# Reordering the passage between two stages of a recurrent layer, and one place for raw weights

## The chip, the cores and the metric

The kernel runs on one core of one Trainium2 chip. The metric is the device time of one execution in microseconds (us). The kernel before takes 1391.1 us, the median of three runs (1390.11 to 1394.08). The engines of the core are named here as in the profile: PE is TensorE (matrix products), DVE is VectorE, ACT is ScalarE, POOL is GpSimd and SP is SyncE. DMA transfers are issued through queues of SP, ACT and POOL. SBUF is the on-chip memory that all engines work on, PSUM the small memory that TensorE writes.

## The reference

The input x has 2048 tokens of 512 numbers. The layer is a gated attention over four lags with a feed-forward gate beside it:

```python
xn = _layernorm(x)
q, k, v = (causal_dwconv(silu(xn @ W), conv_w) for each of q, k, v)   # 16 heads of 128, 4 taps
z, a, b = xn @ Wz, xn @ Wa, xn @ Wb
q, k = rotary(q), rotary(k)
q, k = q / max(norm(q), 1e-12), k / max(norm(k), 1e-12)
out = zeros_like(v)
for s in range(4):                                     # lag s: shifted by s tokens
    attn = einsum('bshd,bshd->bsh', q, lag(k, s)) / sqrt(128)
    gate = sigmoid(lag(a, s) * b)
    out = out + (attn * gate)[..., None] * lag(v, s)
out = out * rsqrt(mean(out * out, over all 2048 channels) + 1e-6) * norm_w * silu(z)
s = out @ Wout
g = silu(relu(xn @ sign(up).T * up_scale) @ sign(down).T * down_scale * output_scale)
x = x + s * g
```

The lines above shorten the reference; every operation is kept.

## The kernel before, in words

Heads are handled in 8 pairs (p, 256 channels each) and tokens in 4 blocks (b, 512 tokens each). The kernel has two stages.

**Stage 1** (to about 760 us) goes over blocks and pairs with one `step` (L508) each: the products of q and k, their convolutions, the rotation (`turn`), the four lagged products of q and k (`product`, into the tiles `pr`), and, as matrix products with a matrix of ones per head, their sums (`sum_dots`) and the sums of squares (`sum_squares`). The feed-forward products (`ups`, `downs`) run beside on TensorE. Once per block, `norms`, `norms_in_rows` and `coefficients` (L470 to L504) make the weights of the four lags for all heads and store them in DRAM as `co_dram[b]`. `norms_in_rows` moves norms between partitions by eight small DMAs on SP's queue (L493, L494), and `coefficients` ends with the store (L504).

**Stage 2** (from about 740 us, main loop at L1056) goes over 16 values of i: 8 pairs for the first 1024 tokens, then 8 for the second 1024. For each i there are

- a projection pv for v (`raw_values`) and a projection pz for z (`gated_outputs`), both through `project_forms`: three products of split operands, first d (16 matmuls), then, after a scaling of the result on ACT (L819), h and m (32 matmuls);
- v's convolution (`values`): ACT makes the first tap (L856), DVE adds three taps for both halves of the channels, six operations;
- for both halves h of the tokens `weighted`: the rows of coefficients are spread over the partitions by DMA (`bc`, four transfers of 256 KB on SP's queue), DVE multiplies them with v (te, twice), adds them, and adds once more to o;
- `gating` (o times silu of z, normed by `norm_w`) and `output_projection` (po) for earlier i.

The weights come as raw 512 KB tiles (`load_raw`, L608), which `split_raw` (L618) divides into three parts: h on ACT (L630), m and d on DVE (L631, L632), then a scaling of m on ACT (L633). Three pools take the parts in turn (`pool_of`, L799): `vs` (opened only after stage 1, L1035), `wp` (the place of stage 1's weights) and `wfp` (the place of the feed-forward's raw weights). v of i is turn 2i, z of i turn 2i + 1. In `vs` and `wfp` a raw tile takes one of the pool's four places of its tag; for `wp` it has a place in `vs` (tag `wraw`).

What sets the order: every instruction issued through `pe`, `dve`, `pool`, `act` and `sp` (the class `InOrder`, L45) keeps the order of the program on its engine or queue; those through `nc.scalar`, `nc.sync` and `nc.gpsimd` are placed by a scheduler, and each engine runs its list in order in the end. Tiles that share a pool's tag share memory: a write waits until the last reader of the tile before is done. `att.close()` (L1033) ends the memory of stage 1's pool `qks`, which `vs` takes over; so the first tiles of `vs` wait for what lies there, such as the coefficients' `rk` and `rq`.

The passage between the stages is written out at L1022 to L1049: the first projection of v, the sums left over from stage 1, `norms` and `norms_in_rows` for the last block, the first projection of z, v's second weights, v's first convolution, `coefficients`, the end of `qks`, two first te tiles, the raw weights of z 1, and the loads of `down_scale` and `out_scale`. The raw weights of v 0 and z 0 are loaded during the last block of stage 1 (p = 4 and p = 6, L780 to L787); z 0 is split inside the last step, between its convolution and its rotation (the argument `between`, L768).

Of the kernel before, what the change touches and what calls it, by code (L numbers as in the profile page):

```python
# [17 lines left out]
P = 128  # L18
# [40 lines left out]
def recurrent_layer(ctx: ExitStack, tc: tile.TileContext, a: dict, out: bass.AP):  # L59
# [40 lines left out]
    wp = ctx.enter_context(tc.tile_pool(name="wp", bufs=3))  # L100
    wfp = ctx.enter_context(tc.tile_pool(name="wfp", bufs=4, side="right"))
# [5 lines left out]
    pr_tiles = [qks.tile([P, LAGS, TB], F32, tag=f"pr{n}", name=f"pr{n}") for n in range(2)] + [spare]  # L107
# [128 lines left out]
    def gate_products(b):  # L236
# [12 lines left out]
        ab = qks.tile([P, TB], F32, tag="ab", name=f"ab_sb{b}", bufs=1)  # L249
# [127 lines left out]
    def queries(p, b):  # L377

        if p or b:
            load("q", p, b)  # L380
        q = qks.tile([P, LAGS, 2, TB], F32, tag="q", name=f"q_{p}_{b}", bufs=1)
        q0 = q[:, LAGS - 1]
        convolve(0, p, raw_of(qks, "q", p, b), q0)
        return q
# [223 lines left out]
    def load_raw(pool, n, i, by=None):  # L608
        if pool is not wp:
            w = pool.tile([P, KC, 2 * P], F32, tag="wf", name=f"w{n}_{i}", bufs=4)  # L610
        elif i:
            w = vs.tile([P, KC, 2 * P], F32, tag="wraw", name=f"w{n}_{i}")
        else:
            w = wfp.tile([P, KC, 2 * P], F32, tag="wf", name=f"w{n}_{i}", bufs=4)
        (by or (sp if i else nc.sync)).dma_start(w, a[f"w{n}"][i % NP])
        w_raws[n, i] = pool, w

    def split_raw(n, i):  # L618
        pool, w = w_raws.pop((n, i))
        h, m, d = (  # L620
            pool.tile(
                [P, KC, 2 * P],
                F32R,
                tag="w" if pool is wp else "wf",
                name=f"w{n}_{i}_{t}",
                bufs=3 if pool is wp else 4,
            )
            for t in "hmd"
        )
# [18 lines left out]
    with tc.tile_pool(name="pre", bufs=1, side="right") as pre:  # L648
# [91 lines left out]
        for b in range(NTB):  # L740
            for p in range(NP):
# [13 lines left out]
                else:  # L755

                    def first_downs():
# [4 lines left out]
                    end = n == len(groups) - 1  # L762
                    step(
                        p,
                        b - 1,
                        first_downs,
                        lambda: downs(b, g, 2, TC),
                        (lambda: split_raw("z", 0)) if end else None,  # L768
                    )
# [9 lines left out]
                if b == NTB - 1:  # L779
                    if p == 4:  # L780
                        load_raw(wfp, "v", 0)
                    if 1 < p < 5:
                        hold_form(0, (2, 0, 1)[p - 2])
                        fill_form(0, (2, 0, 1)[p - 2], nc.sync)
                    if p == 6:
                        split_raw("v", 0)
                        load_raw(wp, "z", 0)  # L787
                        for i in (2, 0, 1):
                            hold_form(1, i)
                            fill_form(1, i, nc.sync)  # L790
# [8 lines left out]
    def pool_of(n, i):  # L799
        return (vs, wp, wfp)[rounds[n, i] % 3]  # L800
# [67 lines left out]
    def weighted(i, h, v):  # L868
        s, p = divmod(i, NP)
        b = 2 * s + h  # L870
        n = f"_{p}_{b}"
        parts = []
        for lo in range(0, LAGS, 2):
            bc = vr.tile([P, 2, TB], F32, tag="bc", name=f"bc{lo}" + n, bufs=3)
            for hd in range(2):
# [27 lines left out]
    def load_wo(i, by=None, tag="wo", bufs=2):  # L903
        wo = take(tag) or (by or vs).tile([P, 2, HID], F32, tag=tag, name=f"wo_{i}", bufs=bufs)
# [65 lines left out]
    def load_squares(s):  # L970
        ss = squares[s] = [
            take("y") or vs.tile([P, TB], F32, tag="y", name=f"ss{s}_{h}", bufs=2) for h in range(2)
# [5 lines left out]
    def roots(s, more=None):  # L978
        so = sums.tile([P, TB], F32, tag="squares", name=f"so{s}")
        row = take("g") or vs.tile([P, TB], F32, tag="g", name=f"row{s}", bufs=2)  # L980
# [40 lines left out]

    raw = raw_values(0)  # L1022
    for work in sums_at.pop(NP * NTB):
        work()
    sum_dots()
    norms(last)
    norms_in_rows(last)
    z0 = gated_outputs(0)
    load_raw(wfp, "v", 1)
    split_raw("v", 1)  # L1030
    v0 = values(0, raw)
# [16 lines left out]
    sp.dma_start(down_scale, a["down_scale"].partition_broadcast(P))  # L1048
    sp.dma_start(out_scale, a["out_scale"].partition_broadcast(P))  # L1049
# [6 lines left out]
    for i in range(n_all + 1):  # L1056
# [23 lines left out]
        if i:  # L1080
# [29 lines left out]
    g_last += [vs.tile([P, 2, HID], F32, tag="wf", name=f"g_last{n}", bufs=4) for n in (2, 3)]  # L1110
# [89 lines left out]
```

## Time and profile before

| what | value |
|---|---|
| median of three runs | 1391.1 us (1390.11 to 1394.08) |
| profiled execution, its own time | 1392.0 us |
| span of the profiled execution | 1390.2 us |
| granted TensorE clock, mean | 0.983 |
| TensorE (PE) busy | 1329.1 us, 96% |
| VectorE (DVE) busy | 1189.0 us, 86% |
| ScalarE (ACT) busy | 841.9 us, 61% |
| GpSimd (POOL) busy | 204.9 us, 15% |
| DMA moved | 285.43 MB, mean 205 GB/s |

The profile page cuts the span into 40 slices of 34.8 us and gives the busy share of each engine as a digit (9 is 90% or more). A line of the timeline is: start in us, duration in us, engine (SPq, ACTq and POOLq are the queues' issues), line, operation, output<-inputs, shapes, the number of instructions joined, and in brackets the idle time of the engine just before with what ended it. A line of the waits is: engine, tile and line that waited, what it waited for, the sum in us, how often, and the longest. Since operations pass through the class `InOrder`, many of them carry its line, L53, and are told apart by their tiles. Buffer numbers are left out of tile names, so `wz_h` is the h part of some z weight.

### The profile page before, as it was taken

What the parts mean: (1) busy time and instruction counts of PE and PEld (TensorE: products, weight loads), DVE (VectorE), ACT (ScalarE), POOL (GpSimd) and SP (SyncE); (2) the same over time, 40 slices, a digit from 0 to 9 for tenths busy, and PEclk for the clock granted to TensorE, in tenths of its full rate; (3) what the DMA queues carried; (4) which work ended last, traced back from release to release, by engine and by line L of the source; (5) the groups of instructions that cost most, each with busy time, mean ns of one, the idle gap of its engine ahead of it and who ended that gap; (6) DMA issues with size and microseconds to landing.
All of it is one profiled execution on the core that took longest, in us unless ns stands there. A gap on an engine that the chain in (4) does not pass through costs nothing. (4 is left out here: it accounts for less than half of the span.)

```text
span 1390.2 us, 13682 instructions
## 1 busy us (share of the span) xinstructions
PE 1329.1 (96%) x4586; PEld 793.0 (57%) x4586; DVE 1189.0 (86%) x1091; ACT 841.9 (61%) x1484; POOL 204.9 (15%) x266
## 2 busy tenths in 40 slices
PE   9999999999999999999997657999999999999996
PEld 6555555555555555555554545666666566666652
DVE  6998999988979888799885489999886898899875
ACT  7566757676577666555655455666655666666541
POOL 1121111112211131111110000111111111111110
PEclk9999999999999999999999879999999999999998
DMA  9969786999889998989784276676889776688876
GB/s 312 359 180 221 191 229 193 217 215 239 228 218 253 221 214 221 255 222 255 169 218 81 76 182 164 151 187 149 181 212 296 173 176 172 180 191 207 206 202 196
DMA packets 100143, 285.43 MB, mean 205 GB/s; under 512 B 16804, under 2 KB 17188, under 8 KB 89576
## 3 DMA queue, kind: packets, MB, share of 16 engines
q1 hardware_dynamic: 66424, 174.43, 41.0%
q0 software_dynamic: 32784, 103.83, 37.8%
q10 hardware_dynamic: 864, 6.29, 1.2%
q8 instruction: 36, 0.59, 0.2%
q14 instruction: 35, 0.29, 0.1%
HBM read 167.05 MB, written 74.47 MB: 174 GB/s over the span
## 5 line engine op out<-in xcount | busy, mean ns | idle before, releaser
L53 PE MATMUL pq<-xn,wq 128*128 128x512 f32 (+1 forms) x528 | 225.6, 580 | 0.6 <-ACT rk L294 0.6
L53 PE MATMUL po<-wo,o 128*128 128x512 f32 x512 | 222.5, 592 | 3.3 <-DVE o L53 3.3
L53 PE MATMUL pk<-xn,wk 128*128 128x512 f32 x512 | 224.9, 592 | 0.0
L53 PEld LDWEIGHTS po<-wo,o 128*128 128x128 f32 x512 | 97.0, 190 | 121.0 <-issue 115.0
L53 PEld LDWEIGHTS pq<-xn,wq 128*128 128x128 f32 x528 | 99.6, 190 | 111.0 <-issue 105.2
L53 PEld LDWEIGHTS pk<-xn,wk 128*128 128x128 f32 x512 | 97.1, 190 | 109.7 <-issue 107.0
L53 DVE SCALAR_TENSOR_TENSOR v<-rv,conv_w,v 128x1024 f32<-128x1024 f32 x96 | 122.0, 1284 | 29.0 <-ACT v L856 26.7
L53 DVE TENSOR_TENSOR te<-v,bc 128x2048 f32<-128x2048 f32 x62 | 139.3, 2287 | 8.5 <-DMA bc<-co_dram 8.1
L53 DVE SCALAR_TENSOR_TENSOR q<-q,turns 128x1024 f32<-128x1024 f32 (+1 forms) x128 | 127.3, 1016 | 4.4 <-ACT q L53 2.2
L53 PE MATMUL pv<-xf,wv_h 128*128 128x512 f32 x256 | 102.2, 399 | 9.6 <-ACT pv L819 9.6
L53 PE MATMUL pf<-down,hid_hi 128*128 128x512 f32 x256 | 108.8, 425 | 0.0
L53 PE MATMUL ph<-xs_h,up 128*128 128x512 f32 x256 | 107.9, 422 | 0.0
L53 PE MATMUL pv<-xf,wv_m 128*128 128x512 f32 x256 | 101.4, 396 | 1.4 <-DMA xf<-forms_dram 1.4
L53 PE MATMUL pf<-down,hid_lo 128*128 128x512 f32 x256 | 100.5, 393 | 0.6 <-DVE hid_lo L53 0.6
L53 PE MATMUL pz<-xf,wz_h 128*128 128x512 f32 x256 | 100.6, 393 | 0.1
L53 DVE SCALAR_TENSOR_TENSOR k<-rk,conv_w,k 128x512 f32<-128x512 f32 x128 | 96.3, 752 | 4.5
L53 DVE SCALAR_TENSOR_TENSOR q<-rq,conv_w,q 128x512 f32<-128x512 f32 x128 | 96.3, 752 | 4.5
L53 PE MATMUL ph<-xs_m,up 128*128 128x512 f32 x256 | 100.0, 391 | 0.0
L53 PE MATMUL pz<-xf,wz_m 128*128 128x512 f32 x256 | 99.9, 390 | 0.0
L53 DVE TENSOR_TENSOR pr<-q,k 128x2048 f32<-128x2048 f32 x44 | 99.6, 2285 | 0.3
L53 PE MATMUL pz<-xf,wz_d 128*128 128x512 f32 x256 | 65.6, 411 | 27.6 <-issue 20.5
L53 DVE SCALAR_TENSOR_TENSOR k<-rk,conv_w,tap 128x512 f32<-128x512 f32 x64 | 48.0, 750 | 48.2 <-ACT tap L360 48.1
(170 smaller groups left out, 2263.0 us busy)
## 6 DMA issues: line engine op xcount, KB each, us to landing
bc<-co_dram SPq DMA_DIRECT2D x128, 256.0 KB
wq<-in_wq_dram SPq DMA_DIRECT2D x32, 512.0 KB
wk<-in_wk_dram SPq DMA_DIRECT2D x32, 512.0 KB
sq<-sq POOLq DMA_DIRECT2D x32, 512.0 KB, 8.3
f_dram<-f POOLq DMA_DIRECT2D x64, 256.0 KB, 8.6
o_dram<-o POOLq DMA_DIRECT2D x30, 512.0 KB, 7.8
s_dram<-part POOLq DMA_DIRECT2D x56, 256.0 KB, 6.5
up<-up_signs SPq DMA_DIRECT2D x12, 1024.0 KB
```

Of the source, the lines that this page charges most:

```text
L53: return self.tc.keep_in_program_order(getattr(self.engine, op)(*args, **kwargs))
```

## The change

- `pr` tiles of stage 1 move from `qks` to `xnp`, a pool that lives on; stage 2's te tiles take their places.
- A new pool `qp` with one place holds q in stage 1, then the three parts of every third weight as one tile (in place of the parts in `vs`), and at the end `g_last` and the last squares of o.
- The raw weights of v 0 and z 0 are loaded at p = 2 of the last block, v 0 is split at p = 5, v 1 is loaded at p = 6. The split of z 0 moves out of the last step to behind it.
- In the passage, v's first convolution, the parts of v 1, the first rows, the first te products (`spread`) and the parts of z 1 come ahead of the coefficients. `weighted` is divided into `load_rows`, `spread` and the rest for this.
- In the main loop, raw weights for `qp` and `wp` go through one place (`wraw` in `vs`, one buffer), loaded by `load_behind` behind the rows of each half. Raw weights for `wfp` are loaded as before.
- `down_scale` and `out_scale` are loaded through ACT's queue instead of SP's. The tile `ab` shares a place with `x_in` (or `gate`), and `take` with its first tiles goes.

```diff
     wp = ctx.enter_context(tc.tile_pool(name="wp", bufs=3))
+    qp = ctx.enter_context(tc.tile_pool(name="qp", bufs=1))
     wfp = ctx.enter_context(tc.tile_pool(name="wfp", bufs=4, side="right"))
...
     spare = xnp.tile([P, LAGS, TB], F32, tag="spare", name="spare")
-    pr_tiles = [qks.tile([P, LAGS, TB], F32, tag=f"pr{n}", name=f"pr{n}") for n in range(2)] + [spare]
+    pr_tiles = [xnp.tile([P, LAGS, TB], F32, tag=f"pr{n}", name=f"pr{n}") for n in range(2)] + [spare]
 
...
             )
-        ab = qks.tile([P, TB], F32, tag="ab", name=f"ab_sb{b}", bufs=1)
+        ab = qks.tile([P, TB], F32, tag="x_in" if b else "gate", name=f"ab_sb{b}", bufs=1)
         nc.scalar.copy(ab, chunks)
...
             load("q", p, b)
-        q = qks.tile([P, LAGS, 2, TB], F32, tag="q", name=f"q_{p}_{b}", bufs=1)
+        q = qp.tile([P, LAGS, 2, TB], F32, tag="q", name=f"q_{p}_{b}")
         q0 = q[:, LAGS - 1]
...
 
-    def load_raw(pool, n, i, by=None):
-        if pool is not wp:
-            w = pool.tile([P, KC, 2 * P], F32, tag="wf", name=f"w{n}_{i}", bufs=4)
-        elif i:
-            w = vs.tile([P, KC, 2 * P], F32, tag="wraw", name=f"w{n}_{i}")
-        else:
-            w = wfp.tile([P, KC, 2 * P], F32, tag="wf", name=f"w{n}_{i}", bufs=4)
-        (by or (sp if i else nc.sync)).dma_start(w, a[f"w{n}"][i % NP])
+    def load_raw(pool, n, i):
+        at, tag, bufs = (wfp, "wf", 4) if pool is wfp else (qks, "x_in", 1) if i < 2 else (vs, "wraw", 1)
+        w = at.tile([P, KC, 2 * P], F32, tag=tag, name=f"w{n}_{i}", bufs=bufs)
+        (sp if i else nc.sync).dma_start(w, a[f"w{n}"][i % NP])
         w_raws[n, i] = pool, w
...
         pool, w = w_raws.pop((n, i))
-        h, m, d = (
-            pool.tile(
-                [P, KC, 2 * P],
-                F32R,
-                tag="w" if pool is wp else "wf",
-                name=f"w{n}_{i}_{t}",
-                bufs=3 if pool is wp else 4,
-            )
-            for t in "hmd"
-        )
+        shape = [P, KC, 2 * P]
+        if pool is qp:
+            parts = qp.tile([P, 3, *shape[1:]], F32R, tag="q", name=f"w{n}_{i}_hmd")
+            h, m, d = (parts[:, t] for t in range(3))
+        else:
+            tag, bufs = ("wf", 4) if pool is wfp else ("w", 3)
+            h, m, d = (pool.tile(shape, F32R, tag=tag, name=f"w{n}_{i}_{t}", bufs=bufs) for t in "hmd")
         nc.scalar.activation(h, w, AF.Copy, scale=LOW)
...
 
-                    end = n == len(groups) - 1
-                    step(
-                        p,
-                        b - 1,
-                        first_downs,
-                        lambda: downs(b, g, 2, TC),
-                        (lambda: split_raw("z", 0)) if end else None,
-                    )
+                    step(p, b - 1, first_downs, lambda: downs(b, g, 2, TC))
                 if n + 1 < len(groups):
...
                 if b == NTB - 1:
-                    if p == 4:
+                    if p == 2:
                         load_raw(wfp, "v", 0)
+                        load_raw(wp, "z", 0)
                     if 1 < p < 5:
...
                         fill_form(0, (2, 0, 1)[p - 2], nc.sync)
-                    if p == 6:
+                    if p == 5:
                         split_raw("v", 0)
-                        load_raw(wp, "z", 0)
+                    if p == 6:
+                        load_raw(wfp, "v", 1)
                         for i in (2, 0, 1):
...
     def pool_of(n, i):
-        return (vs, wp, wfp)[rounds[n, i] % 3]
+        return (qp, wp, wfp)[rounds[n, i] % 3]
 
...
 
-    def weighted(i, h, v):
+    def load_rows(i, h):
         s, p = divmod(i, NP)
         b = 2 * s + h
-        n = f"_{p}_{b}"
-        parts = []
+        bcs = []
         for lo in range(0, LAGS, 2):
-            bc = vr.tile([P, 2, TB], F32, tag="bc", name=f"bc{lo}" + n, bufs=3)
+            bc = vr.tile([P, 2, TB], F32, tag="bc", name=f"bc{lo}_{p}_{b}", bufs=3)
+            bcs.append(bc)
             for hd in range(2):
...
                 )
+        return bcs
+
+    def spread(i, h, v, bcs):
+        s, p = divmod(i, NP)
+        n = f"_{p}_{2 * s + h}"
+        parts = []
+        for lo, bc in zip(range(0, LAGS, 2), bcs):
             v0 = v[:, :, h * TB + lo : h * TB + lo + TB]
             v_lags = bass.AP(v0.tensor, v0.offset, [v0.ap[0], [1, 2], *v0.ap[1:]])
-            te = take(f"te{lo}") or vs.tile([P, 2, 2, TB], F32, tag=f"te{lo}", name=f"te{lo}" + n)
+            te = xnp.tile([P, 2, 2, TB], F32, tag=f"pr{lo // 2}", name=f"te{lo}" + n)
             dve.tensor_tensor(te, v_lags, bc.unsqueeze(2).to_broadcast([P, 2, 2, TB]), ALU.mult)
...
         dve.tensor_tensor(parts[0], parts[0], parts[1], ALU.add)
-        o = take("oz") or vs.tile([P, 2, TB], F32, tag="oz", name="o" + n, bufs=6)
-        dve.tensor_tensor(o, parts[0][:, 0], parts[0][:, 1], ALU.add)
+        return parts[0]
+
+    def weighted(i, h, part):
+        s, p = divmod(i, NP)
+        b = 2 * s + h
+        n = f"_{p}_{b}"
+        o = vs.tile([P, 2, TB], F32, tag="oz", name="o" + n, bufs=6)
+        dve.tensor_tensor(o, part[:, 0], part[:, 1], ALU.add)
         os[i, h] = o
         if h and i == NSB * NP - 1:
-            o2 = vs.tile([P, 2, TB], F32, tag="wf", name="o2" + n, bufs=4)
+            o2 = end_places[2]
         else:
...
 
+    split_raw("z", 0)
     raw = raw_values(0)
...
     sum_dots()
+    load_raw(qp, "z", 1)
     norms(last)
-    norms_in_rows(last)
     z0 = gated_outputs(0)
-    load_raw(wfp, "v", 1)
-    split_raw("v", 1)
     v0 = values(0, raw)
+    split_raw("v", 1)
+    first_rows = [load_rows(0, h) for h in range(2)]
+    norms_in_rows(last)
+    first_part = spread(0, 0, v0, first_rows[0])
+    split_raw("z", 1)
     coefficients(last)
...
     vs = ctx.enter_context(tc.tile_pool(name="vs", bufs=1))
-    firsts = {}
-
-    def first(tag, shape, name, bufs=1):
-        firsts[tag] = vs.tile(shape, F32, tag=tag, name=name, bufs=bufs)
-
-    def take(tag):
-        return firsts.pop(tag, None)
-
-    first("te0", [P, 2, 2, TB], "te0_first")
-    first("te2", [P, 2, 2, TB], "te2_first")
-    load_raw(pool_of("z", 1), "z", 1)
     down_scale = vs.tile([P, HID], F32, tag="down_scale", name="down_scale")
-    sp.dma_start(down_scale, a["down_scale"].partition_broadcast(P))
-    sp.dma_start(out_scale, a["out_scale"].partition_broadcast(P))
+    nc.scalar.dma_start(down_scale, a["down_scale"].partition_broadcast(P))
+    nc.scalar.dma_start(out_scale, a["out_scale"].partition_broadcast(P))
+
+    def load_behind(n, i):
+        if i < 2 or i >= n_all or pool_of(n, i) is wfp:
+            return
+        for _ in range(2):
+            n, i = ("z", i) if n == "v" else ("v", i + 1)
+            if i < n_all and pool_of(n, i) is not wfp:
+                load_raw(pool_of(n, i), n, i)
+                return
 
...
                 split_raw("v", i + 1)
-            if i + 2 < n_all:
+            if i + 2 < n_all and pool_of("v", i + 2) is wfp:
                 load_raw(pool_of("v", i + 2), "v", i + 2)
...
             load_raw(pool_of("v", 2), "v", 2)
+        if i == n_all - 1:
+            ends = qp.tile([P, 4, 2, HID], F32, tag="q", name="ends")
+            end_places = [ends[:, n] for n in range(3)]
         v = values(i, raw) if i else v0
         for h in range(2):
-            weighted(i, h, v)
+            rows_of_h = load_rows(i, h) if i else first_rows[h]
+            load_behind("vz"[h], i + 1)
+            weighted(i, h, spread(i, h, v, rows_of_h) if i or h else first_part)
             if ended:
...
                 load_end(2 * (i - NP - 3) + h)
-            if not h and i + 1 < n_all:
+            if not h and 0 < i < n_all - 1:
                 split_raw("z", i + 1)
-            if not h and i + 2 < n_all:
+            if not h and i + 2 < n_all and pool_of("z", i + 2) is wfp:
                 load_raw(pool_of("z", i + 2), "z", i + 2)
...
     ]
-    g_last += [vs.tile([P, 2, HID], F32, tag="wf", name=f"g_last{n}", bufs=4) for n in (2, 3)]
+    g_last += end_places[:2]
     parts = []
```

Where `take(...) or` stood before a tile, the tile alone is left.

More of the change, by code (lines that the diff above doesn't have):

```diff
@@ L784, in recurrent_layer @@
                         fill_form(0, (2, 0, 1)[p - 2], nc.sync)
+                    if p == 5:
+                        split_raw("v", 0)
                     if p == 6:
-                        split_raw("v", 0)
-                        load_raw(wp, "z", 0)
+                        load_raw(wfp, "v", 1)
                         for i in (2, 0, 1):
@@ L903, in load_wo @@
     def load_wo(i, by=None, tag="wo", bufs=2):
-        wo = take(tag) or (by or vs).tile([P, 2, HID], F32, tag=tag, name=f"wo_{i}", bufs=bufs)
+        wo = (by or vs).tile([P, 2, HID], F32, tag=tag, name=f"wo_{i}", bufs=bufs)
         sp.dma_start(wo, a["wo"][i % NP])
@@ L971, in load_squares @@
         ss = squares[s] = [
-            take("y") or vs.tile([P, TB], F32, tag="y", name=f"ss{s}_{h}", bufs=2) for h in range(2)
+            vs.tile([P, TB], F32, tag="y", name=f"ss{s}_{h}", bufs=2) for h in range(2)
         ]
@@ L979, in roots @@
         so = sums.tile([P, TB], F32, tag="squares", name=f"so{s}")
-        row = take("g") or vs.tile([P, TB], F32, tag="g", name=f"row{s}", bufs=2)
+        row = vs.tile([P, TB], F32, tag="g", name=f"row{s}", bufs=2)
         ss = squares.pop(s)
@@ L1025, in recurrent_layer @@
     sum_dots()
+    load_raw(qp, "z", 1)
     norms(last)
+    z0 = gated_outputs(0)
+    v0 = values(0, raw)
+    split_raw("v", 1)
+    first_rows = [load_rows(0, h) for h in range(2)]
     norms_in_rows(last)
-    z0 = gated_outputs(0)
-    load_raw(wfp, "v", 1)
-    split_raw("v", 1)
-    v0 = values(0, raw)
+    first_part = spread(0, 0, v0, first_rows[0])
+    split_raw("z", 1)
     coefficients(last)
```

## Prediction

> **What bounds the kernel now.** I read the page's busy shares first, then its 40 slices, then TensorE's waits, then the timelines of the engines that those waits name.
>
> ```profile
> PE 1329.1 (96%) x4586; PEld 793.0 (57%) x4586; DVE 1189.0 (86%) x1091; ACT 841.9 (61%) x1484; POOL 204.9 (15%) x266
> ...
> PE   9999999999999999999997657999999999999996
> ```
>
> TensorE works 1329.1 of 1390.2 us. The 61 us that it stands idle lie almost all in slices 22 to 24, which is 740 to 850 us, the passage from stage 1 (queries and keys) to stage 2 (values and gates). The waits of TensorE between 740 and 860 us give their causes:
>
> ```profile
> PE pz L53 <- issue: 20.5, 1, 20.5
> PE pz L53 <- DVE wz_d L53: 7.1, 1, 7.1
> PE pv L53 <- ACT pv L819: 7.0, 1, 7.0
> PE pv L53 <- DVE wv_d L53: 5.9, 1, 5.9
> ```
>
> Four gaps, 40.5 us together. After each the clock is low for a while: sixteen matmuls of one form take 6.11 us after the long gap, 3.93 us without one, in the timeline of TensorE:
>
> ```profile
> 814.72 6.11 PE L53 MATMUL pz<-xf,wz_d 128*128 128x512 f32 x16 [20.53 <-issue]
> 828.03 3.93 PE L53 MATMUL pv<-xf,wv_d 128*128 128x512 f32 x16
> ```
>
> So a gap of seven or more microseconds costs about 2.2 us (6.11 - 3.93) on top. The Trainium skill ("TensorE: Matmul & The Clock Gate", part 1 on the clock gate) has the array at half clock until it has been busy for about 3.4 us; by that rule the surcharge would be an estimated 1.7 us per gap, and the total below would move by about 1 us. I use the row.
>
> What stands behind the gaps is seen on ScalarE, VectorE and SyncE's queue:
>
> ```profile
> 736.14 1.06 ACT L630 ACTIVATE wz_h<-wz 128x1024 fp32r<-128x1024 f32 x1 [7.68 <-DMA wz<-in_wz_dram]
> ...
> 808.58 1.06 ACT L630 ACTIVATE wz_h<-wz 128x1024 fp32r<-128x1024 f32 x1 [6.15 <-DMA wz<-in_wz_dram]
> ...
> 1073.93 1.06 ACT L630 ACTIVATE wv_h<-wv 128x1024 fp32r<-128x1024 f32 x1 [4.33 <-DMA wv<-in_wv_dram]
> ```
>
> ```profile
> 790.15 0.33 SPq L504 DMA_DIRECT2D co_dram<-rk  x1
> ...
> 796.93 0.64 SPq L53 DMA_DIRECT2D wz<-in_wz_dram  x1
> ```
>
> ```profile
> 803.74 2.29 DVE L53 TENSOR_TENSOR te_first<-v,bc 128x2048 f32<-128x2048 f32 x1 [13.62 <-DMA bc<-co_dram]
> ```
>
> The coefficients' last work holds memory that stage 2 needs. Only when they are stored (790.15) are the rows and z's second raw weights loaded. VectorE then stands for 13.62 us, and z's second parts are ready only at 814.6.
>
> **The change, part by part.** The program orders of the two kernels, with the durations of these rows, give the following.
>
> (1) z's first raw weights are loaded four steps earlier, and only h is made before the last products. The wait of 7.68 us ahead of wz_h goes, as does that wz_h (1.06 us) from ScalarE's way to rk's eviction, and 2.45 us (1.22 + 1.23) of m and d on VectorE from before the turn. The products end near 746 instead of 756.3. TensorE's 7.02 us and its ramp go: v's first projection ends near 751 instead of 760.0. The loads themselves I cost at nothing, since they lie beside slices in which PE reads 9 and are used steps later; without that cover each would cost the 3.5 us of a load on a quiet queue (v's second weights, issued 773.46, used 776.94).
>
> (2) v's second raw weights come two steps before the end instead of behind eight rq/rk issues, so their parts (1.06 + 1.23 + 1.22 us) are ready near 765 instead of 780.5. The 5.90 us wait and its ramp go: pv 1 runs from about 765.5 to 777.
>
> (3) z's second parts go to the third place, freed by the last products. VectorE, with r's reciprocal done at 768.6, does two te products and their sum (3 x 2.29 = 6.9) to 775.5, then m and d (2.45) to 778. pz 1 starts near 778 instead of 814.72: the 20.53 us gap shrinks to about 1.
>
> (4) The coefficients now come behind this. Five of the eight rq/rk issues stand on SyncE behind a row load that waits for the first te. The three coefficient operations (3 x 0.68) end near 781.5, the store takes 2.0 us, and only then is there memory for o and for the raw weights of v 2 and z 2. VectorE from 783.5: o 1.2, te of the second half with sum and o 8.0, two gatings 2.5, parts of v 2 2.5, v 1's convolution 7.8, te and o of the next half 8.0, parts of z 2 2.5. That sums to 816.0. With two short waits for the loads I take 818 for the start of pz 2, against 846.29 (the gap of 7.1 us there ends with VectorE's d). Here is the whole gain of the passage: **28 us**. It is no more, since a gap of some 9.5 us is left ahead of pv 2, whose weights wait for the store. Bounds: 34, if the store needs no wait for the rq/rk copies; 18, if the last rq/rk copy and the raw weights each land like the slowest load shown (11.65 us, issued 796.93, used 808.58).
>
> (5) From there TensorE bounds again: per pair 11.1 (pz) + 13.7 (po) + 11.1 (pv) = 35.9 us against 31.2 us on VectorE. Nothing of this is removed, so the gain stays unless the new loads take some of it back.
>
> (6) The raw weights of two of the three places now go through one place, each issued behind the rows of a half. At i = 2, 5, 8, 11 and 14 it is z(i+1), split in the same i. SyncE waits until v(i+1)'s m has been taken (952.15 at i = 5), and ScalarE has wz_h in order ahead of the scalings of pz, for which TensorE waits. Before, that load had a whole pair of time. At i = 5 the row is kind: a weight load issued at 952.24 had its 0.5 MB through by 956 to 957 (SyncE's DMA queue moved 0.47 MB from 952 to 956 us and 0.54 MB in the next two), and the scalings are needed by 959.83. Nothing lost. At i = 11 I put 1 us, at i = 14 2 us, with two output weights in the queue (2.05 us of issue); bounds 0 and 10 together.
>
> (7) At i = 8, the change of super-block, it isn't kind:
>
> ```profile
> 1052.85 11.40 SPq L53 DMA_DIRECT2D ss<-o_dram  x2
> 1064.36 0.45 SPq L53 DMA_DIRECT2D wv<-in_wv_dram  x1
> 1064.87 2.56 SPq L53 DMA_DIRECT2D bc<-co_dram  x4
> 1067.52 0.55 SPq L53 DMA_DIRECT2D wz<-in_wz_dram  x1
> ```
>
> ```profile
> 1076.59 2.29 DVE L53 TENSOR_TENSOR te<-v,bc 128x2048 f32<-128x2048 f32 x1 [3.52 <-DMA bc<-co_dram]
> 1079.57 2.29 DVE L53 TENSOR_TENSOR te<-v,bc 128x2048 f32<-128x2048 f32 x1 [0.69 <-DMA bc<-co_dram]
> ```
>
> SyncE is held by the sums of squares until 1064.36, then come v's weights and four rows, and the rows land at 1076.59 and 1079.57. z's load behind them, at 1067.52, thus lands near 1081. In before it is a weight of two pairs later, so nobody waits; in after it is z 9, and wz_h stands ahead of the scalings of pz 8, whose d part ends on TensorE at 1069.2. wz_h to 1082, a scaling 0.6: TensorE stands from 1069.2 to 1082.7, 13.5 us, and ramps for 2.2. VectorE, bound there by the rows, isn't delayed, so the 2.59 us that TensorE waited at 1097.65 go: **net 13.1 us lost**. Bounds: 2 (the 3.5 us of the quiet load) and 18 (landing 5 us later). I take the middle of the chain because all its rows are of this very place. The Trainium skill ("DMA: Bandwidth & Descriptors", rules for kernel authors) wants loads issued early and waited for late, which speaks against this part; it gives no price, and the two waiting te rows here agree with it.
>
> (8) Costed at nothing: down_scale and out_scale on ScalarE's queue instead of SyncE's (0.43 + 0.44 us). down_scale waits there for the store of the coefficients, near 783.5, and the next in ScalarE's order, the square of o, needs an o that comes later still; without that cover 0.9. Likewise ab in x_in's place, the products' tiles in another pool, the end's tiles in the third place (same instructions and the same queue order; the tail's 3.34 us wait for o stays).
>
> Sum on the profiled execution, 1392.0 us (span 1390.2): 1392.0 - 28 + 13.1 + 3 = 1380.1. The median of the runs is 0.9 lower, hence **1379**.
>
> **The rivals.** (a) The load of z 9 is hidden, by a queue that serves it beside the rows: 1391 - 28 + 2 + 3 = 1368, or 1391 - 34 + 2 = 1359 with every bound at its kind end. For it speaks the quiet load of 3.5 us; against it the two te waits at just that place. (b) VectorE's chain bounds the passage with late copies: gain 18 to 22, then 1391 - 20 + 16 = 1387 (1383 to 1392). For it, the slowest loads there (11.65) and the five issues behind a waiting one; against it, DMA is 0.19 to 0.34 busy between 740 and 800 us. (c) Slower: the one raw place holds ScalarE at every tight pair. If a load took 11.65 us at each of the other four, it would land at 963.9, TensorE would stand till 965.6, 5.7 us past 959.83, plus 2.2: 4 x 7.9 + 13.1 = 44.7 lost, 1391 - 28 + 44.7 = 1408. It decides from 3.7 us at each, a latency of 7.4 us (28 = 4 x 3.7 + 13.1). For it: 7.8 and 11.65 us behind rows; against it: 4 to 5 us at i = 5. (d) The change does not do what it says: then 1391; the built order shows that the moves happen.
>
> **How the numbers follow.** Chances: mine, 1373 to 1385, 0.52; (a) 0.18; (b) 0.17; (c) 0.12; (d) 0.01. A measurement tells 0.3%, about 4.2 us: faster is under 1387. Mine, (a) and half of (b) lie there: 0.79. Same: the other half and (d), 0.09. Slower 0.12. The range leaves out (c) and the low end of (a): 1360 to 1393; the likeliest's own is 1373 to 1385.
>
> **What would show it.** Right: TensorE without the waits on wv_d and on issue before 800 us, one gap of 8 to 11 us ahead of pv 2, pz 2 near 818; at i = 8, near 1041 (1069.2 - 28), a stall of 10 to 16 us in pz, and on ScalarE a wz_h that waits for the DMA of wz just before its end. Wrong: VectorE waiting for o's memory past 790, a pz wait at i = 5, 11 or 14, or none at i = 8. The forecast fails most easily by the size of that one stall, or if a load of stage 1 is held up.

## The result and the profile after

The changed kernel takes 1397.28 us (median of 8 runs, 1393.89 to 1400.74) against 1391.38 us for the kernel before beside it. The ratio is 1.0042, with a 95% interval of 1.0027 to 1.0057: **slower by 0.42%**, where 1379 us were forecast. The profiled execution has a span of 1395.8 us against 1390.2.

The page's busy shares and 40 slices of the changed kernel:

```profile
PE 1334.1 (96%) x4586; PEld 795.6 (57%) x4586; DVE 1189.2 (85%) x1091; ACT 842.0 (60%) x1484; POOL 204.8 (15%) x266
...
PE   9999999999999999999999789999996999997997
```

The broad hollow of the passage has shrunk to a 7 and an 8 (23rd and 24th digit, from 768 us). Two others have come, the 31st digit (from 1047 us) and the 37th (from 1256 us), and the busy time has grown by 5 us: after the new gaps the clock is lower (granted 0.50 from 1059.4 to 1063 us, right behind the 31st slice's gap; 1.00 from 1055 to 1100 in the kernel before), and the matmuls there take longer. The waits of TensorE over the whole execution of the changed kernel (tile, line, releaser, sum in us, times, longest):

```profile
PE pz L53 <- ACT pz L808: 26.0, 6, 11.3
PE pv L53 <- DVE wv_d L53: 9.5, 1, 9.5
PE pz L53 <- DVE wz_d L53: 4.2, 1, 4.2
```

The 20.5 us on issue and the 5.9 us on v's parts are gone; 26 us of pz waiting for ACT's scalings (L808, which was L819) are new. The timeline of TensorE in the changed kernel gives the places:

```profile
778.00 11.17 PE L53 MATMUL pz<-xf,wz_hmd 128*128 128x512 f32 x48 [0.70 <-DVE wz_hmd L53]
798.68 6.75 PE L53 MATMUL pv<-xf,wv_d 128*128 128x512 f32 x16 [9.50 <-DVE wv_d L53]
816.94 6.22 PE L53 MATMUL pz<-xf,wz_d 128*128 128x512 f32 x16 [4.22 <-DVE wz_d L53]
...
1059.36 0.79 PE L53 MATMUL pz<-xf,wz_h 128*128 128x512 f32 x1 [11.30 <-ACT pz L808]
...
1291.52 0.80 PE L53 MATMUL pz<-xf,wz_h 128*128 128x512 f32 x1 [10.63 <-ACT pz L808]
```

The last of the passage's three rows, pz 2 at 816.94, has this row in the timeline of the kernel before:

```profile
846.29 5.75 PE L53 MATMUL pz<-xf,wz_d 128*128 128x512 f32 x16 [7.08 <-DVE wz_d L53]
```

pz 2 starts at 816.94 instead of 846.29, so the passage did win 29.35 us. Where they went is read from the start of each projection in the two timelines, the changed kernel less the kernel before:

| start of | difference, us | lost since the row above |
|---|---|---|
| pz 2 | -29.35 | |
| pv 5 | -27.68 | 1.7, spread |
| pv 6 | -23.56 | 4.1, at z 6 (i = 5) |
| pv 8 | -23.54 | 0 |
| pv 10 | -9.29 | 14.25, at z 9 (i = 8) |
| pv 12 | -9.07 | 0.2, at z 12 (i = 11) |
| pv 14 | -6.89 | 2.2, at i = 12 and 13 |
| pv 15 | +5.89 | 12.8, at z 15 (i = 14) |

The two large losses look alike on ScalarE. The lines of its timeline (the first is the smaller loss, z 6):

```profile
930.59 1.06 ACT L624 ACTIVATE wz_h<-wz 128x1024 fp32r<-128x1024 f32 x1 [3.26 <-DMA wz<-in_wz_dram]
...
1057.77 1.06 ACT L624 ACTIVATE wz_h<-wz 128x1024 fp32r<-128x1024 f32 x1 [11.61 <-DMA wz<-in_wz_dram]
...
1289.92 1.06 ACT L624 ACTIVATE wz_h<-wz 128x1024 fp32r<-128x1024 f32 x1 [9.98 <-DMA wz<-in_wz_dram]
1290.88 2.04 ACT L808 ACTIVATE pz<-pz 128x512 f32<-128x512 f32 x4
```

ScalarE stands 10 to 12 us for raw weights that are used a pair later, and the four scalings that TensorE needs now come right behind. SyncE's queue at i = 14 shows what the load of z 15 has in front:

```profile
1273.41 1.05 SPq L53 DMA_DIRECT2D wo<-in_wo_dram  x2
1274.52 2.69 SPq L53 DMA_DIRECT2D bc<-co_dram  x4
1277.31 0.64 SPq L53 DMA_DIRECT2D wz<-in_wz_dram  x1
```

Two output weights and four rows, 2 MB, were issued in the four microseconds before; the 0.5 MB of z 15 were usable 12.6 us after their issue (1277.31 to 1289.92). TensorE had done the d part of pz 14 at 1280.89 (1291.52 less the wait of 10.63), so only 3.6 us were free for the load. From 1277 to 1289 us SyncE's queue moved 3.1 MB and GpSimd's 0.26 MB.

### The profile page after: what moved, and what is told of

It is laid out like the page before. It is cut to its first block, busy times and chain, and to the rows that moved or that the text cites. A ratio compares the mean times of both kernels' runs of the same rounds, so it can differ in the third digit from the quotient of the medians.

```text
span 1395.8 us, 13681 instructions
## 1 busy us (share of the span) xinstructions
PE 1334.1 (96%) x4586; PEld 795.6 (57%) x4586; DVE 1189.2 (85%) x1091; ACT 842.0 (60%) x1484; POOL 204.8 (15%) x266
## 5 line engine op out<-in xcount | busy, mean ns | idle before, releaser
L53 DVE TENSOR_TENSOR te<-v,bc 128x2048 f32<-128x2048 f32 x64 | 143.7, 2285 | 8.2 <-DMA bc<-co_dram 7.8
L53 PE MATMUL pz<-xf,wz_h 128*128 128x512 f32 x176 | 73.5, 417 | 25.4 <-ACT pz L808 25.4
L348 ACT ACTIVATE rq<-pq 128x512 f32<-128x512 f32 x62 | 37.2, 600 | 86.8 <-PE pq L53 86.5
L348 ACT ACTIVATE rk<-pk 128x512 f32<-128x512 f32 x64 | 38.3, 598 | 77.5 <-PE pk L53 77.3
L421 POOL DMA_DIRECT2D sq<-sq x32 | 30.9, 967 | 297.6 <-ACT sq L53 169.1
L53 DVE TENSOR_TENSOR te<-te,te 128x2048 f32<-128x2048 f32 x32 | 73.3, 2292 | 1.1
```

The source lines that it names most:

```text
L53: return self.tc.keep_in_program_order(getattr(self.engine, op)(*args, **kwargs))
L348: nc.scalar.activation(to[:, j, :], pp, AF.Silu)
L421: nc.gpsimd.dma_start(sq[0], sq[1], accum_op=ALU.add)
```

## Experiments

My theory after the comparison: the passage gives its 29 us, and they are given back because the one raw place makes five loads late, with ScalarE in order behind them. The rivals: the loss in stage 2 is DMA traffic or VectorE's work whatever is loaded; or the late load is on the path whoever waits for it. Ratios are to the kernel before, run on the same chip.

### 1. Two raw places, each load one step earlier

Against the changed kernel:

```diff
-    w_ab = const.tile([P, KC, LW], F32, name="w_ab")
+    w_ab = qks.tile([P, KC, LW], F32, tag="w_ab", name="w_ab")
...
-        at, tag, bufs = (wfp, "wf", 4) if pool is wfp else (qks, "x_in", 1) if i < 2 else (vs, "wraw", 1)
+        at, tag, bufs = (wfp, "wf", 4) if pool is wfp else (qks, "x_in", 1) if i < 2 else (vs, "wraw", 2)
...
-            part = vr.tile([P, HID], F32, tag="part", name=f"part{c}_{i}_{h}", bufs=4)
+            part = vr.tile([P, HID], F32, tag="part", name=f"part{c}_{i}_{h}", bufs=3)
...
+    behind = [(n, i) for i in range(2, n_all) for n in "vz" if pool_of(n, i) is not wfp]
+
     def load_behind(n, i):
-        if i < 2 or i >= n_all or pool_of(n, i) is wfp:
-            return
-        for _ in range(2):
-            n, i = ("z", i) if n == "v" else ("v", i + 1)
-            if i < n_all and pool_of(n, i) is not wfp:
-                load_raw(pool_of(n, i), n, i)
-                return
+        if (n, i) in behind and behind.index((n, i)) + 2 < len(behind):
+            n, i = behind[behind.index((n, i)) + 2]
+            load_raw(pool_of(n, i), n, i)
...
-            load_raw(pool_of("v", 2), "v", 2)
+            for n, k in behind[:2]:
+                load_raw(pool_of(n, k), n, k)
```

> The changed kernel with two raw places of 4 KB instead of one (the memory comes from one fewer buffer of part, 3 instead of 4, and from w_ab moved out of the constants), each raw weight of the two pools loaded one place of the sequence earlier, so that z 6, z 9, z 12 and z 15 have a whole pair of time. Theory: the passage keeps its 29 us, and the late loads cost 4.1 (z 6) + 13.4 (z 9, net) + 2 (z 12) + 13.1 (z 15) us, so this kernel takes 1397.3 - 32 = 1365 us (1360 to 1372), with no wait of pz for ACT above 2 us. Rival: the loss in stage 2 comes from DMA traffic or from VectorE and not from the one place: then it stays between 1390 and 1398.

Measured: 1371.47 us, ratio 0.9857 (0.9837 to 0.9876). The long waits of pz are gone, so the rival falls. The time is 6 us above the theory's, and there is a new wait, which the edit itself made (experiment 5 shows it). The first line is from ScalarE's timeline of this kernel:

```profile
1040.42 0.59 ACT L960 COPY part<-po 128x512 f32<-128x512 f32 x1 [7.86 <-DMA s_dram<-part]
```

and the second from TensorE's:

```profile
1041.55 0.80 PE L53 MATMUL pv<-xf,wv_h 128*128 128x512 f32 x1 [6.18 <-ACT pv L808]
```

The copy of an output chunk waits for one of the three buffers of part, and pv's scaling stands behind it.

### 2. The split of the late weights written later

```diff
-            if not h and 0 < i < n_all - 1:
+            if not h and 0 < i < n_all - 1 and (i + 1) % 3:
                 split_raw("z", i + 1)
...
             gating(i - 1, gated_outputs(i - 1))
+        if i and i % 3 == 0 and i < n_all:
+            split_raw("z", i)
```

> The changed kernel with the loads where they are, but the split of z 3, z 6, z 9, z 12 and z 15 written behind the gating of the pair before, so that wz_h comes behind the scalings of pz in ScalarE's order. Theory (a late load hurts only because ScalarE stands in order ahead of what TensorE needs): the loads are as late as before, but the waits of 11.3 and 10.6 us of pz go, 1366 to 1375 us. Rival (the load itself is on the path, whoever waits for it): the stalls move to pz of the next pair, 1390 to 1400 us.

Measured: 1398.86 us, ratio 1.0057 (1.0035 to 1.008), as slow as the changed kernel. This decides nothing between the two, since the edit did not do what it says. ScalarE's timeline of this kernel at i = 8:

```profile
1050.17 1.07 ACT L808 ACTIVATE pz<-pz 128x512 f32<-128x512 f32 x2
1063.37 1.06 ACT L624 ACTIVATE wz_h<-wz 128x1024 fp32r<-128x1024 f32 x1 [12.13 <-DMA wz<-in_wz_dram]
1064.34 1.06 ACT L808 ACTIVATE pz<-pz 128x512 f32<-128x512 f32 x2
```

The scheduler placed wz_h in the middle of the four scalings, where two of them still wait for it.

### 3. The kernel before with z 0's split behind the last step

```diff
-                    step(
-                        p,
-                        b - 1,
-                        first_downs,
-                        lambda: downs(b, g, 2, TC),
-                        (lambda: split_raw("z", 0)) if end else None,
-                    )
+                    step(p, b - 1, first_downs, lambda: downs(b, g, 2, TC))
...
+    split_raw("z", 0)
     raw = raw_values(0)
```

> The kernel before with one part of the change alone: the split of z 0 moves from inside the last step to behind the loop; loads stay where they were. Theory: ScalarE's wait of 7.68 us for z 0's raw weights no longer holds back the last keys, the gap of 7.0 us of TensorE at 743 goes and all that follows shifts by 9 to 10 us: 1381 to 1383 us. Rival: the passage is set by the coefficients and the loads behind them, and no more than 3 us are won: 1388 to 1391 us.

Measured: 1386.72 us, ratio 0.9961 (0.9946 to 0.9976): 4.5 us won, between the two expectations. pv 1 starts 4.5 and pv 2 5.5 us earlier. Again the program's place was not the place on ScalarE:

```profile
735.30 1.06 ACT L630 ACTIVATE wz_h<-wz 128x1024 fp32r<-128x1024 f32 x1 [7.53 <-DMA wz<-in_wz_dram]
736.27 0.58 ACT L347 ACTIVATE rk<-pk 128x512 f32<-128x512 f32 x1
```

wz_h still waits ahead of the last keys; only m and d went behind VectorE's products. So the move of the split is worth 4.5 us by itself. The wait of 7.5 us stays with it; in the changed kernel, where the load is early too, it is gone.

### 4. The coefficients ahead again

```diff
     norms(last)
+    norms_in_rows(last)
     z0 = gated_outputs(0)
     v0 = values(0, raw)
     split_raw("v", 1)
+    coefficients(last)
     first_rows = [load_rows(0, h) for h in range(2)]
-    norms_in_rows(last)
     first_part = spread(0, 0, v0, first_rows[0])
     split_raw("z", 1)
-    coefficients(last)
```

> The changed kernel with the norms in rows and the coefficients put ahead of the first rows, the first te products and the parts of z 1 again (the rest of the change stays, so no memory of stage 1 is waited for by te or the parts of z 1). Theory (what counts is that z 1's parts and te have places that do not wait for the store, not the order): within 4 us of the changed kernel, 1393 to 1400 us. Rival (the order itself brings the gain): the gap ahead of pz 1 comes back by 10 to 20 us, 1407 to 1417 us.

Measured: 1405.75 us, ratio 1.0106 (1.0091 to 1.0121), 8.5 us slower than the changed kernel: outside both expectations. VectorE's timeline names the reason:

```profile
780.45 4.59 DVE L53 TENSOR_TENSOR te<-v,bc 128x2048 f32<-128x2048 f32 x2 [6.39 <-DMA bc<-co_dram]
```

The rows stand on SyncE behind the store of the coefficients, which waits for VectorE. I had moved the rows behind the coefficients without counting their place on that queue. Experiment 11 takes this apart.

### 5. Two places, and part with its four buffers

Against experiment 1; `ident`, `of_head` and three tiles of `kept` are used in stage 1 alone:

```diff
-    ident = const.tile([P, P], F32, name="ident")
-    of_head = const.tile([P, NP, LW], F32, name="of_head")
...
-    kept = {n: const.tile([P, NP, 2, HALO], F32, name=f"kept_{n}") for n in ("rq", "rk", "rv", "k", "v")}
+    kept = {n: const.tile([P, NP, 2, HALO], F32, name=f"kept_{n}") for n in ("rv", "v")}
...
+    ident = qks.tile([P, P], F32, tag="ident", name="ident")
+    of_head = qks.tile([P, NP, LW], F32, tag="of_head", name="of_head")
+    kept |= {n: qks.tile([P, NP, 2, HALO], F32, tag=f"kept_{n}", name=f"kept_{n}") for n in ("rq", "rk", "k")}
...
-            part = vr.tile([P, HID], F32, tag="part", name=f"part{c}_{i}_{h}", bufs=3)
+            part = vr.tile([P, HID], F32, tag="part", name=f"part{c}_{i}_{h}", bufs=4)
```

> As the first experiment, but the memory for the second raw place comes from small tiles of stage 1 that move out of the constants (w_ab, ident, of_head, three kept tiles), and part keeps its four buffers. In the first experiment TensorE waited 6.18 us at 1041.55 for ACT, which waited 7.86 us for a buffer of part to be stored. Theory: this wait and its ramp were made by the fourth buffer alone, so 1371.5 - 6.2 - 1 to 2 = 1364 us (1361 to 1367). Rival: the wait is the store's own lateness at the change of super-block and stays: 1370 to 1373.

Measured: **1364.9 us** (1364.26 to 1365.81), ratio 0.9805 (0.979 to 0.982), the best of all and 26 us below the kernel before. The waits of TensorE:

```profile
PE pv L53 <- DVE wv_d L53: 9.1, 1, 9.1
PE pz L53 <- DVE wz_d L53: 5.7, 1, 5.7
PE po L53 <- DVE o L53: 4.7, 1, 4.7
PE pz L53 <- ACT pz L809: 2.3, 3, 1.2
```

pz 2 starts 28.05 us earlier than in the kernel before and pz 15 still 27.42: of the passage's gain, 0.6 us are lost on the way. What is left are the gaps of the passage and the tail.

### 6. The scalings and wz_h in the program's order

Against experiment 2; the last argument is the issuer of h:

```diff
-            nc.scalar.mul(pp, pp, -1.0 / (UNIT + 1.0))
+            act.mul(pp, pp, -1.0 / (UNIT + 1.0))
...
-            split_raw("z", i)
+            split_raw("z", i, act)
```

> As the second experiment, but the scalings of pz and pv and wz_h of the five late weights are issued in the program's order on ScalarE, so that wz_h comes behind all four scalings and the evictions of z. In the second experiment wz_h still stood after two of the four scalings, and the stall stayed. Theory (only ScalarE's order makes a late load costly): the waits of pz of 9 to 11 us go though the loads land as late as before, 1366 to 1376 us. Rival (the late parts hold up VectorE or the next pz as much): 1388 to 1400 us.

Measured: 1734.17 us, ratio 1.2458 (1.244 to 1.2477). This experiment failed as a test: the scalings of every pair came behind all that the program has before them, the squares of o among it, and TensorE waited at fifteen pairs:

```profile
PE pz L53 <- ACT pz L53: 363.5, 15, 43.8
```

It does show what this kernel pays when pz's scalings stand behind other work on ScalarE.

### 7. Two places, every load at its old slot

Against the changed kernel, with the memory of experiment 5:

```diff
-        at, tag, bufs = (wfp, "wf", 4) if pool is wfp else (qks, "x_in", 1) if i < 2 else (vs, "wraw", 1)
+        at, tag, bufs = (wfp, "wf", 4) if pool is wfp else (qks, "x_in", 1) if i < 2 else (vs, "wraw", 2)
```

> The changed kernel with two raw places, but every load at the slot of the program where it was. Theory: at i = 8 and i = 14 the place was long free, and what delays the load is its slot on SP's queue behind four rows, so both stalls stay; only z 6's load, which waited for the place, comes earlier and its 4.1 us go: 1393 us (1390 to 1396). Rival (the single place itself is what costs): 1364 to 1372 us, as with loads one step earlier.

Measured: 1394.74 us, ratio 1.003 (1.0017 to 1.0042). Its interval touches that of the changed kernel, so at most a few microseconds came from the place. The stalls stayed, as the theory has it: 14.55 us are lost between pv 8 and pv 10, 9.1 at i = 14. One detail went otherwise: z 6's loss stayed too (4.64 us from pv 5 to pv 6), although its load was issued at 914.59 instead of 923.37. SyncE's queue of this kernel has it behind v's weights and four rows:

```profile
909.73 0.33 SPq L53 DMA_DIRECT2D wv<-in_wv_dram  x1
910.16 4.38 SPq L53 DMA_DIRECT2D bc<-co_dram  x4
914.59 0.60 SPq L53 DMA_DIRECT2D wz<-in_wz_dram  x1
```

ScalarE used it only at 927.42, after a wait of 5.85 us, 12.8 us after the issue. So it is not the second place by itself but the earlier slot that experiment 1 won with. (An earlier slot with one place was not run; there the load would have to wait for the place.)

### 8. Only z 15's load one slot earlier

Against experiment 7:

```diff
                 if i < n_all and pool_of(n, i) is not wfp:
-                    load_raw(pool_of(n, i), n, i)
+                    if (n, i) != ("z", 15):
+                        load_raw(pool_of(n, i), n, i)
+                    if (n, i) == ("v", 15):
+                        load_raw(pool_of("z", 15), "z", 15)
```

> As the one before in this set, with only z 15's raw load moved one slot ahead (right behind v 15's). Theory: of the losses z 15's 13.1 us go on top of z 6's 4.1, the stall of pz at i = 8 stays: 1380 us (1377 to 1384). Rival (the stall at i = 14 comes from the output weights and the ends' traffic whatever is loaded): 1391 to 1395 us.

Measured: 1384.56 us, ratio 0.9954 (0.9938 to 0.9969), 10.2 us below experiment 7. The starts of pv 14 and pv 15 against the kernel before are -9.83 and -10.14: nothing is lost at i = 14 any more, and i = 8 is as bad as it was. One slot is nearly a whole pair: the load is issued at 1236.79, and ScalarE uses it at 1269.33 without a wait. So the experiment shows that the load's lateness made the stall; which of the transfers in front of it made it late, it does not separate. (The expectation had counted z 6 as won.)

### 9. wz_h of the late weights on GpSimd

```diff
-        nc.scalar.activation(h, w, AF.Copy, scale=LOW)
+        if n == "z" and i and i % 3 == 0:
+            nc.gpsimd.tensor_scalar(h, w, LOW, None, ALU.mult)
+        else:
+            nc.scalar.activation(h, w, AF.Copy, scale=LOW)
```

> The changed kernel, loads and places as they are, but wz_h of z 3, z 6, z 9, z 12 and z 15 is computed on GpSimd instead of ScalarE. So the five late loads are as late as before, and only ScalarE no longer stands in order behind them (forcing the order by the program, as in the experiment before, put all scalings behind the squares of o and cost 337 us, which tells nothing of this). Theory (a late load costs because ScalarE waits for it ahead of the scalings of pz): the waits of pz of 11.3 and 10.6 us go or shrink below 3, 1366 to 1380 us. Rival (VectorE, which needs wz_h for m in its order, carries the lateness on to TensorE): 1388 to 1400 us.

Measured: 1369.22 us, ratio 0.9845 (0.983 to 0.986). One raw place, the same slots, the same late loads, and 28 us less than the changed kernel. The lateness is still there, on GpSimd:

```profile
1054.34 4.08 POOL L625 TENSOR_SCALAR wz_h<-wz 128x1024 fp32r<-128x1024 f32 x1 [10.06 <-DMA wz<-in_wz_dram]
...
1271.01 3.83 POOL L625 TENSOR_SCALAR wz_h<-wz 128x1024 fp32r<-128x1024 f32 x1 [16.17 <-DMA wz<-in_wz_dram]
```

and harms nobody: h takes 3.8 to 4.1 us there instead of 1.06, and TensorE's waits of pz for ACT sum to 1.7 us. The five operations that left ScalarE are 5.3 us of its work (5 x 1.06), too little for 28. This settles it between theory and rival: the load costs because ScalarE waits for it in order ahead of pz's scalings; VectorE and the next pz have room for it.

### 10. Only z 9's load one slot earlier

The edit of experiment 8 with 9 in place of 15.

> The kernel with two places and every load at its old slot (1394.7 us), with only z 9's raw load moved one slot ahead. Theory: the 13.9 us between pv 8 and pv 9 that are lost there against the kernel before go, the 2 to 3 us of rows that VectorE waits for stay: 1394.7 - 14 + 1 = 1382 us (1379 to 1386). Rival (the change of super-block is slow by its own traffic): 1391 to 1396 us.

Measured: 1381.81 us, ratio 0.9933 (0.9916 to 0.9949), 12.9 us below experiment 7. From pv 8 to pv 10 the start against the kernel before moves from -20.32 to -20.61, so that stretch loses nothing. The two single repairs, 10.2 and 12.9 us, are most of the 29.8 us that lie between experiments 7 and 5.

### 11. The rows first, then the coefficients

```diff
     norms(last)
+    norms_in_rows(last)
...
-    first_rows = [load_rows(0, h) for h in range(2)]
-    norms_in_rows(last)
+    first_rows = [load_rows(0, 0)]
+    coefficients(last)
+    first_rows.append(load_rows(0, 1))
     first_part = spread(0, 0, v0, first_rows[0])
     split_raw("z", 1)
-    coefficients(last)
```

> The order of the passage once more: as the fourth experiment (coefficients ahead of the first te products and of the parts of z 1), but the rows of the first half are loaded ahead of the coefficients' store. In the fourth experiment the rows stood behind the store on SP and VectorE waited 6.39 us for them. Theory (the order of the rows on SP's queue made the loss there, the order of the coefficients on VectorE does not matter): pz 1 comes near 783 instead of 778.0, pv 2 at 797 to 800 as in the changed kernel, and the time is within 3 us of 1397.3. Rival (the coefficients ahead of te and z 1's parts cost by themselves): 1403 to 1407 us.

Measured: 1397.62 us, ratio 1.0045 (1.003 to 1.006), the changed kernel's time. pz 1 comes at 784.74, pv 2 at 800.58. pz 2 starts 29.35 us before that of the kernel before in the changed kernel, 27.44 here and 20.76 in experiment 4. So the rows' place on SyncE made 6.7 of the 8.6 us that experiment 4 lost in the passage, and the coefficients' place on VectorE at most 1.9. (That the whole time is equal is in part chance: between pv 14 and pv 15 this run lost 9.6 us, the changed kernel 12.8.) What counts most is that te and z 1's parts do not wait for the store. That their memory is free without it counts as well is read from the order of the kernel before; no run here tests it alone.

### 12. The same on the best kernel

> The same order on the fifth experiment's kernel (two places, loads one step earlier, part with four buffers; 1364.9 us). Theory: within 3 us of 1364.9. Rival: 6 to 10 us slower, 1371 to 1375 us.

Measured: 1366.73 us, ratio 0.9818 (0.9802 to 0.9835): 1.8 us above experiment 5, and the two intervals overlap.

## Why the prediction was wrong, step by step

- **Steps 1 to 4, the passage: right.** Forecast pz 1 at 778, pz 2 at 818 and a gap of some 9.5 us ahead of pv 2; measured 778.00, 816.94 and 9.50. 28 us were forecast, 29.35 came. Experiment 5, which loses almost nothing later, ends 26 us below the kernel before.
- **Step 5, the gain stays in the steady state: nearly right.** 1.7 us were lost by i = 5 without a wait of note.
- **Step 7, z 9: right in its mechanism, and the closeness of the sum in part luck.** 13.1 us net were forecast; 14.25 were lost there, with wz_h at 1057.77 behind a DMA wait of 11.61 us. The load took 13.56 us from issue (1044.21) to use, as good as the 13.5 of the forecast (1067.52 to 1081). From pz 8 to pv 9, 13.7 us were lost where 15.7 were forecast (13.5 and the ramp of 2.2), and 2.9 came back behind it (2.6 forecast). But 2.6 more were lost ahead of pz 8, which I had not forecast: TensorE's wait there for xf was 2.09 us instead of 1.36, and behind it eight matmuls took 0.60 to 0.63 us each, which took 0.39 in the kernel before. Experiment 10 shows that the loss goes with that one load.
- **Step 6, the other late loads: this is the step that failed.** I gave z 15 at i = 14 2 us; it cost 12.8. I charged the two output weights with the time of their issue (2.05 us) and not with their 1 MB, which goes through the same queue ahead of the load, as do four rows. I had counted this for i = 8, where the rows ahead were seen to be late, and not for i = 14, although the same kinds of rows stood in the kernel before on SyncE at that pair, two output weights and then the four rows. The bound of 10 us for i = 11 and 14 together was too low for the same reason. (That these bytes made the load late fits the 3.1 MB that the queue moved until its use; it was not tested apart from the other traffic.) The mechanism, ScalarE in order behind a late load, was right; the term that was mis-sized is the latency of the load, which measured 12.6 us with 3.6 us free for it.
- **Step 6, z 6 at i = 5:** forecast 0, lost 4.1. The load had 7.2 us from issue (923.37) to use (930.59), not the 4 to 5 that I took from one load of the same kind in the kernel before. No instruction waited for that one, so its landing was inferred from the bytes of the queue and not seen. The wait on ScalarE was 3.26 us, TensorE's 2.29, and the clock had to come back (single matmuls of 0.63 us behind the wait, then 0.39).
- **Step 6, z 12:** forecast 1 us; at most 0.2 were lost at i = 11. ScalarE waited 2.65 us for the load and used it at 1165.60, 4.8 us before the scalings of pz 11 (1170.39). The 2.2 us lost at i = 12 and 13 were in no step of mine; TensorE waited there for the scalings of pv (1.29 us at 1197.44, 0.56 at 1233.89), and what made these late was not tested.
- The sum, measured less forecast: 10.8 (z 15) + 4.1 (z 6) - 0.8 (z 12) + 2.2 (i = 12 and 13) + 1.7 (spread) + 1.2 (z 9) - 1.4 (the passage) = 17.8 us, against 1397.3 - 1379 = 18.3 measured.
- **The rivals.** The one that ended slower, (c), came nearest, with the threshold that I gave: 28 us are lost when the four other loads cost 3.7 us each, 14.9 together. They cost 12.8, 4.1, 0.5 and 0.2, 17.6 together. But it was not "every tight pair", one load made most of it; and by experiment 7 the load is late by its slot, hardly by the one place. I thought of them as one kind with one latency and took the kindest pair's row as evidence for all four. Rival (b) did not happen: the gain was 29.35 us and not 18 to 22, and VectorE waited 2.15 us for the store. VectorE's chain does set the end of the passage, as step 4 had it: pv 2 and pz 2 both wait for VectorE (9.50 and 4.22 us).
- **Step 8** needed no price: no wait on down_scale, ab or the ends is among TensorE's waits in the changed kernel. In step 1, experiment 3 adds that pz 0 starts 6.2 us earlier by the move of the split alone; it is 8.6 us in the changed kernel, with the early load.
- **Two readings of rows were off**, though no term of the sum rests on them. The load at 796.93 and the wz_h at 808.58 are those of z 2, not of z's second weights. These (z 1) were issued at 792.25 and their h was made at 795.85; their m came only at 812.14, since it stands on VectorE behind the te products that waited for the rows. And the load of 7.8 us (793.58 to 801.38) that rival (c) has behind rows was issued ahead of them, behind z 1's weights and the two scales.

## What to carry to other kernels

When a prefetch is made later, price each of its places by itself: list what is in front of it on its DMA queue in bytes, not in issues, what the other queues move at the time, and which instructions stand behind the first user on that user's engine. Where the user is an engine that also feeds the bottleneck in order, a load that is 10 us late costs those 10 us (9.98 us of ScalarE's wait at i = 14, 10.63 of TensorE's); on an engine with time to spare it cost next to nothing (experiment 9). A gain that is won in one stage can only be believed to the end when the loads of the later stages are as early as they were.

## What the runs showed of the hardware

A load of 0.5 MB was usable 3.5 us after its issue on a quiet queue (the kernel before, 773.46 to 776.94), and 12.6 and 12.8 us after it behind 1.5 to 2 MB of rows and weights on the same queue (i = 14 of the changed kernel, i = 5 of experiment 7). The queue's own bytes are not all: v 9's load of the kernel before took 9.6 us (issued 1064.36, used 1073.93 after a wait of 4.33) with two loads of 256 KB right in front of it, while from 1064.3 to 1074 GpSimd's queue moved 0.98 MB beside the 1.51 MB of SyncE's; the two shares were not tested apart. The same multiplication of 128x1024 elements by a constant, with fp32r output, took 1.06 us on ScalarE and 2.8 to 4.1 us on GpSimd. I had not expected the scheduler to leave an instruction ahead of work that the program has before it (experiments 2 and 3): an edit of the program's order has to be looked for on the engine's own list.
